# Turning each token tile's table places into integers one tile at a time, in an attention and mixture-of-experts kernel

## The chip, the cores and the metric

The kernel runs on one core of a Trainium2 chip. The metric is the device time of one launch in microseconds (us), from inputs in DRAM to the output in DRAM. The engines are TensorE (PE in the profile; its weight loads are shown apart as PEld), VectorE (DVE), ScalarE (ACT), GpSimd (POOL) and SyncE (SP). SP only issues transfers; POOL does a few element-wise steps and issues the indirect transfers, which are the scatters and gathers by a list of row numbers.

## What is computed

One transformer layer over x of shape (2, 1024, 256), all in float32: cross-attention to 154 context rows with 16 heads of 16, then a feed-forward with 8 experts, of which each token takes its two best.

```python
x = x + xattn(layernorm(x), ctx, ctx)          # 16 heads, softmax over 154 keys, then @ Wo + bo
z = layernorm(x)
probs = softmax(z @ router_w.T)                # 8 experts
vals, idx = top_k(probs, 2)
for e in range(8):
    w = sum(where(idx == e, vals, 0))          # 0 for tokens that did not choose e
    y = gelu(z @ w1[e].T) @ w2[e].T            # 256 -> 1024 -> 256
    out += w[:, None] * y
x = x + out
```

The kernel computes an expert only for the tokens that chose it.

## The kernel before

The 2048 tokens are 16 token tiles of 128, kept as four blocks n = 0..3 of four tiles i = 0..3 (TB = 4). The attention goes block by block; the expert stage goes over expert tiles j, each of which holds up to 128 (token, choice) pairs of one expert. There are 36 unconditional expert tiles (NI) and three more behind a test at the end.

**A written order.** The work is cut into small parts, generators such as `maxima(n, k)` or `expand(j, half)`, and every `yield` ends a piece of one. The string ORDER (lines 45 to 131) names the parts one after the other; each time a name comes up, that part goes on by one piece (line 1115). The instruction order of PE, DVE, ACT and SP is the order in which ORDER issues them. POOL's is too, until the part `release`; after it the scheduler of the framework chooses POOL's order. A queue is worked off in order, so an instruction that waits holds up all behind it on its own engine.

**Attention of one block**: `maxima` (PE scores, DVE row maxima, line 621), `drop` (DVE transposes the maxima, line 635; SP writes them to DRAM and from there into q, lines 638 and 641), `exps` and `last_exps` (PE scores, ACT exponentials, lines 653 to 674), `values` (PE, then a DVE transposition, line 695), `divide` (DVE reciprocal, product, transposition, lines 702 to 712), `project` (PE by Wo, DVE addition, SP store to out), `second_moments`, `second_scale`, `second_norm` (DVE, ACT, and an SP store of the normed rows to `x2n_d`).

**Routing of one block**: `logits` (PE, DVE, ACT), `share` and `choose` (DVE ranks the experts of each token), `place(n)` (PE counts the tokens ahead, DVE computes for each token and choice a row number in a table, lines 832 to 847). At its end `place` turns all eight row numbers per partition of the block into integers with one instruction (line 845). `record(n, i)` (line 849) then issues, for token tile i, one scatter for each of the two choices: 128 entries of token number and weight go to rows of the table `tab_d` in DRAM (line 854). The sixteen records are 32 scatters.

**Experts**: `plan(1)` counts after blocks 0 and 1 how many tiles each expert surely has, and with that fixes tiles 0 to 8; `plan(0)` fixes the rest after all blocks. Per tile j: `entries` (SP loads 128 table rows; it must follow the scatters), `fetch_weights` (SP, two loads of 512 KB), `fetch_rows` (POOL gathers the normed rows, line 973), `flip_rows` (PE transposes them, DVE copies, line 985), `expand` in two halves (PE, then gelu on ACT, line 1002), `contract` in two halves (PE, DVE weighting at line 1020, POOL scatter with addition into out, line 1023). The experts' second weights come by `load_w2(e)`, 1 MB each, on SP. After ORDER is used up, `tiles(0, NI)` issues what remains, tile by tile.

PSUM is shared: tag "one" has two buffers (among them those of logits, project, place, plan, values, flip_rows, contract), tag "two" has three (maxima, exps, last_exps, expand). A PE part can't begin before the buffer that it takes has been read out by DVE or ACT.

## Time and profile before

| what | value |
|---|---|
| median of 6 runs | 471.15 us (466.86 to 473.01) |
| profiled execution, its own time | 468.42 us |
| its span, first to last instruction | 466.7 us |
| granted PE clock, mean over the span | 0.961 |
| PE busy | 433.2 us (93%) |
| DVE, ACT, POOL busy | 169.6, 125.2, 149.2 us |
| scatters to the table (line 854) | 32, 975 ns each on POOL |
| integer conversions (line 845) | 4, 171 ns each |
| expand, contract on PE (lines 997, 1013) | 140.3 and 130.4 us in all |

A row of the timeline gives the start, the duration, the engine, the line, the operation, the tiles (out<-in) and how often; in brackets the idle time of that engine just before and what ended it. "remote" there means that the profile found no instruction that ended the wait. A row of the windows view gives, for a stretch of the span, each engine's busy time with its number of instructions, then the granted PE clock (1.00 is full speed), the share of the transfer engines and the rate.

### The profile page before, as it was taken

The numbers are of one execution on the slowest core, as the hardware profiler recorded it, in microseconds if no ns is written. First come the engines' busy times: TensorE is split into PE (matmuls) and PEld (weight loads), VectorE is DVE, ScalarE is ACT, GpSimd is POOL, SyncE is SP. The second block draws the span as 40 slices with busy tenths as digits, with TensorE's granted clock in tenths as the row PEclk, the third lists the DMA queues.
The fourth block names the chain that finished last, engine by engine and source line by source line (L and its number), as shares of the span: only waits on it lengthen the run. The fifth ranks groups of instructions, "written<-read, shape, count | busy, mean of one in ns | idle before, by whom it ended". The sixth has DMA issues, their size and how long they took to land. (4 is left out here: it accounts for less than half of the span.)

```text
span 466.7 us, 8169 instructions
## 1 busy us (share of the span) xinstructions
PE 433.2 (93%) x2992; PEld 334.9 (72%) x2992; DVE 169.6 (36%) x435; ACT 125.2 (27%) x206; POOL 149.2 (32%) x166
## 2 busy tenths in 40 slices
PE   7999999999985998979699999999999999999991
PEld 6554555344343427969699989999999999999990
DVE  6757766878842746631410111111111111111100
ACT  3275453441541450610111112111121111211210
POOL 5030242000075012466534334333343333432221
PEclk9999999999897598999999999999999999999997
DMA  8301222021714265968368765766656656662211
GB/s 268 132 8 27 86 97 95 9 93 46 305 27 91 73 199 158 249 117 308 47 176 258 213 197 141 200 163 182 207 136 196 174 161 208 148 192 25 23 14 13
DMA packets 32121, 63.75 MB, mean 137 GB/s; under 512 B 11929, under 2 KB 17617, under 8 KB 31057
## 3 DMA queue, kind: packets, MB, share of 16 engines
q1 hardware_dynamic: 23664, 54.19, 36.6%
q0 software_dynamic: 7936, 8.43, 10.8%
q8 instruction: 26, 0.43, 0.4%
q10 hardware_dynamic: 481, 0.58, 0.4%
q14 instruction: 14, 0.11, 0.1%
HBM read 54.63 MB, written 9.60 MB: 138 GB/s over the span
## 5 line engine op out<-in xcount | busy, mean ns | idle before, releaser
L997 PE MATMUL hp<-xgT,w 128*128 128x128 f32 x1152 | 140.3, 280 | 8.3 <-DVE xgT L985 4.7
L997 PEld LDWEIGHTS hp<-xgT,w 128*128 128x128 f32 x1152 | 137.6, 195 | 11.9 <-DVE xgT L985 5.9
L1013 PE MATMUL yp<-w_sb,hT 128*128 x576 | 130.4, 379 | 0.0
L1013 PEld LDWEIGHTS yp<-w_sb,hT 128*128 128x128 f32 x576 | 106.7, 190 | 13.1
L1002 ACT ACTIVATE hT<-hp 128x512 f32<-128x512 f32 x72 | 42.5, 597 | 224.7 <-issue 105.1
L1023 POOL DMA_INDIRECT out_dram<-ag,ents x36 | 57.2, 1589 | 106.4 <-DVE ag L1020 88.3
L973 POOL DMA_INDIRECT xg<-x2n_d,ents x36 | 38.0, 1055 | 85.9 <-PE xgt L982 48.2
L621 DVE TENSOR_REDUCE nmx<-mx 128x4 f32<-128x616 f32 x64 | 48.5, 793 | 32.2 <-PE mx L614 20.4
L1020 DVE TENSOR_SCALAR ag<-yp,ents 128x256 f32<-128x256 f32 x36 | 17.4, 483 | 114.5 <-PE yp L1013 78.5
L985 DVE COPY xgT<-xgt 128x256 f32<-128x256 f32 x36 | 15.2, 423 | 106.3 <-PE xgt L982 96.8
L854 POOL DMA_INDIRECT tab_d<-entry,rows_i x32 | 31.2, 975 | 37.6 <-issue 34.6
L659 ACT ACTIVATE et<-st 128x1024 f32<-128x1024 f32 x32 | 31.7, 1024 | 42.7 <-PE st L653 37.4
L614 PE MATMUL mx<-kaug,q 32*128 32x154 f32 x512 | 33.5, 330 | 9.0 <-issue 5.2
L614 PEld LDWEIGHTS mx<-kaug,q 32*128 32x128 f32 x512 | 23.7, 192 | 24.5 <-issue 11.3
L653 PE MATMUL st<-q,kaug 32*128 32x512 f32 x128 | 23.2, 665 | 0.4 <-DVE nmx L621 0.4
L684 PE MATMUL av<-er,vrem 128*128 128x512 f32 x32 | 19.7, 701 | 0.0
L596 POOL TENSOR_TENSOR x_sb<-x_sb,bo 128x1024 f32<-128x1024 f32 x4 | 9.4, 2356 | 27.0 <-DVE bo L548 25.9
L689 PE MATMUL av<-et,vaug 128*32 128x512 f32 x128 | 17.9, 633 | 0.0
L721 PE MATMUL op<-wo,catT 128*128 128x256 f32 x64 | 17.5, 422 | 0.0
L668 PE MATMUL sr<-q,krem 128*128 128x512 f32 x32 | 17.4, 672 | 0.0
L982 PE MATMUL xgt<-ident,xg 128*128 128x128 f32 x72 | 13.8, 273 | 2.6 <-DMA xg<-x2n_d,ents 2.6
L354 PE MATMUL qp<-w_sb,wq 128*128 128x512 f32 x32 | 16.0, 623 | 0.0
(169 smaller groups left out, 273.7 us busy)
## 6 DMA issues: line engine op xcount, KB each, us to landing
w<-in_w_dram SPq DMA_DIRECT2D x72, 512.0 KB
w_sb<-in_w_dram SPq DMA_DIRECT2D x8, 1024.0 KB
out_dram<-x_sb SPq DMA_DIRECT2D x8, 256.0 KB
x2n_d<-x2n SPq DMA_DIRECT2D x8, 256.0 KB
x_sb<-in_x_dram SPq DMA_DIRECT2D x3, 512.0 KB
ents<-tab_d SPq DMA_DIRECT2D x36, 1.0 KB
xg<-x2n_d,ents POOLq DMA_INDIRECT x36
out_dram<-ag,ents POOLq DMA_INDIRECT x36
```

What stands on the lines that cost most here:

```text
L614: nc.tensor.matmul(sc[j // 2][:, j % 2, gg * SC : (gg + 1) * SC], q[r, gg, i * P : (i + 1) * P], kaug[r, b, 2 * c + gg, :], start=True, st ...
L621: nc.vector.tensor_reduce(out=nmx[c][:, i, 0 : 2 * QJ].rearrange("p (g j) -> p j g", g=2)[:, pair * 2 : pair * 2 + 2, :], in_=sc[pair][:, ...
L653: nc.tensor.matmul(st[j // 2][:, j % 2, :], kaug[r, b, g, 0:SM], q[r, g % 2, :], start=True, stop=True)
L659: nc.scalar.activation(et, st[pair], AF.Exp)
L684: nc.tensor.matmul(av, vrem[:, b, g].rearrange("p j k -> p (j k)"), state["er", n, half][:, gg, :], start=True, stop=False,)
L689: nc.tensor.matmul(av[j * QR : (j + 1) * QR, :], vaug[:, b, g, j, :], state["et", n, g, j // 2][:, j % 2, :], start=False, stop=True,)
L854: ins = nc.gpsimd.indirect_dma_start(out=tab_d, out_offset=bass.IndirectOffsetOnAxis(ap=rows_i[:, i, k : k + 1], axis=0), in_=entry[:, n * ...
L973: nc.gpsimd.indirect_dma_start(out=xg[j % 3], out_offset=None, in_=x2n_d[0 : reach(j), :], in_offset=row_of(j), bounds_check=reach(j) - 1, ...
L997: nc.tensor.matmul(hp[:, q, :], w1t[dc][:, hc * P : (hc + 1) * P], xgT[:, dc, :], start=dc == 0, stop=dc == DC - 1,)
L1002: nc.scalar.activation(hT[:, half * (HC // 2) : (half + 1) * (HC // 2), :], hp, AF.Gelu)
L1013: nc.tensor.matmul(yp, hT[:, hc, :], flat[:, bass.ds(e * (HC * D) + hc * D, D)], start=hc == 0, stop=hc == HC - 1,)
L1023: nc.gpsimd.indirect_dma_start(out=out[0 : reach(j), :], in_=ag[j % 3], in_offset=None, out_offset=row_of(j), bounds_check=reach(j) - 1, o ...
```

## The change

`place` no longer converts the row numbers. Each `record(n, i)` begins with a DVE instruction of its own that converts the two row numbers of its token tile, and ends with the two scatters as before; the tile of unconverted numbers gets two buffers. There are thus 16 small conversions for 4 larger ones, and each has a place of its own in ORDER. All parts stand in a new order. The names and numbers of the other parts and their computation stay the same. Of the two ORDER strings, the stretches around the records are shown; in the new one a record appears twice, first for its conversion, then for its scatters.

```diff
@@ -43,91 +43,93 @@
 ORDER = """
...
-second_norm.0 maxima.3.3 drop.3.0 last_exps.2.1 last_exps.2.1 load_w2.6 exps.2.3 load_w2.7
-values.2.2 load_w2.4 share.1 second_norm.0 share.1 exps.2.3 drop.3.0 place.0 record.0.0 share.1
-exps.2.3 values.2.2 choose.1 values.2.3 choose.1 place.1 exps.3.0 values.2.3 record.0.1
-record.0.2 second_scale.1 last_exps.3.0 exps.3.0 exps.3.0 last_exps.3.0 divide.2.1 divide.2.1
-maxima.3.4 project.2.0 record.0.3 place.1 maxima.3.4 second_norm.1 project.0.1 maxima.3.5
-record.1.0 maxima.3.4 project.2.0 second_norm.1 project.2.1 maxima.3.5 maxima.3.6 maxima.3.5
-second_moments.2.0 add_bias.3 record.1.1 second_moments.2.0 project.2.1 plan.1 maxima.3.6
-maxima.3.6 project.1.1 second_norm.0 exps.3.1 exps.3.1 second_moments.2.1 record.1.2 maxima.3.7
-second_moments.2.1 second_norm.0 second_norm.1 second_scale.2 project.2.0 second_norm.1
-maxima.3.7 project.2.1 second_scale.2 record.1.3 second_norm.2 maxima.3.7 second_norm.2
-second_norm.2 exps.3.1 drop.3.1 drop.3.1 second_norm.2 plan.1 values.3.0 values.3.0 values.3.1
-logits.2 plan.1 fetch_weights.0 logits.2 exps.3.2 exps.3.2 values.3.1 exps.3.2 last_exps.3.1
-entries.0 entries.1 logits.2 exps.3.3 divide.3.0 last_exps.3.1 fetch_rows.0 exps.3.3 values.3.2
-exps.3.3 values.3.3 values.3.2 fetch_rows.1 divide.3.0 entries.4 flip_rows.0 flip_rows.0
-values.3.3 divide.3.1 logits.2 entries.6 divide.3.1 fetch_weights.1 entries.3 expand.0.0
-flip_rows.1 expand.0.1 expand.0.1 entries.8 project.3.0 entries.2 share.2 share.2 fetch_rows.3
-entries.5 flip_rows.1 share.2 fetch_rows.2 project.3.0 logits.3 expand.1.0 expand.1.0
-flip_rows.2 logits.3 choose.2 project.3.1 fetch_weights.2 flip_rows.2 choose.2 expand.0.0
-entries.7 project.3.1 second_moments.3.1 contract.0.0 second_moments.3.0 contract.0.1 place.2
-project.3.0 second_moments.3.1 fetch_weights.3 second_moments.3.0 expand.1.1 second_scale.3
-fetch_weights.7 contract.0.1 second_scale.3 second_norm.3 flip_rows.3 place.2 expand.2.0
-logits.3 logits.3 record.2.0 share.3 second_norm.3 record.2.1 expand.2.1 share.3 share.3
...
+choose.0 choose.0 last_exps.2.0 values.1.3 maxima.2.4 flip_half.3.0 maxima.2.4 maxima.2.5
+flip_half.3.1 flip_half.3.0 maxima.2.5 maxima.2.5 maxima.2.6 maxima.2.6 place.0 place.0
+record.0.0 maxima.2.6 record.0.0 flip_half.3.1 add_bias.1 exps.2.1 prep_q.3.0 exps.2.1
+divide.1.1 exps.2.1 prep_q.3.0 divide.1.1 maxima.2.7 maxima.2.7 maxima.2.7 drop.2.1 project.1.0
+project.1.0 prep_q.3.0 second_moments.1.0 second_moments.1.0 maxima.3.0 values.2.0 maxima.3.0
+project.0.0 maxima.3.1 maxima.3.0 maxima.3.1 record.0.1 project.1.1 maxima.3.1 values.2.0
+project.1.1 drop.2.1 exps.2.2 logits.1 exps.2.2 second_norm.0 second_moments.1.1 maxima.3.2
+exps.2.2 second_moments.1.1 values.2.1 second_scale.1 logits.1 maxima.3.2 maxima.3.3 logits.1
+load_w2.5 maxima.3.2 record.0.1 record.0.2 values.2.1 maxima.3.3 maxima.3.3 divide.2.0 logits.1
+last_exps.2.1 drop.3.0 divide.2.0 prep_q.3.1 share.1 share.1 exps.2.3 load_w2.6 record.0.2
+record.0.3 last_exps.2.1 values.2.2 second_scale.1 drop.3.0 share.1 values.2.2 second_norm.0
+prep_q.3.1 exps.2.3 choose.1 prep_q.3.1 exps.2.3 second_norm.1 values.2.3 choose.1 place.1
+exps.3.0 place.1 record.0.3 values.2.3 exps.3.0 exps.3.0 record.1.0 add_bias.2 divide.2.1
+divide.2.1 last_exps.3.0 maxima.3.4 record.1.0 second_norm.0 last_exps.3.0 maxima.3.4
+own_logits.3 own_logits.3 maxima.3.5 second_norm.1 load_w2.1 maxima.3.4 maxima.3.5 maxima.3.5
+record.1.1 project.1.0 project.2.0 project.2.0 maxima.3.6 maxima.3.6 plan.1 exps.3.1 record.1.1
+maxima.3.6 plan.1 logits.2 exps.3.1 maxima.3.7 project.2.1 maxima.3.7 maxima.3.7 add_bias.3
+record.1.2 drop.3.1 second_norm.1 second_moments.2.0 load_w2.3 logits.2 project.2.1
+second_moments.2.0 exps.3.1 values.3.0 second_moments.2.1 second_moments.2.1 values.3.0
+second_scale.2 second_scale.2 record.1.2 second_norm.1 load_w2.7 second_norm.2 values.3.1
+drop.3.1 exps.3.2 values.3.1 record.1.3 second_norm.2 second_norm.2 logits.2 exps.3.2 exps.3.2
+last_exps.3.1 plan.1 last_exps.3.1 second_norm.2 record.1.3 exps.3.3 fetch_weights.0 exps.3.3
+logits.2 divide.3.0 values.3.2 exps.3.3 entries.0 divide.3.0 fetch_rows.0 values.3.3 entries.2
+fetch_rows.2 entries.1 values.3.2 values.3.3 divide.3.1 entries.8 entries.6 divide.3.1 share.2
+share.2 project.3.0 fetch_rows.1 project.3.1 project.3.0 share.2 flip_rows.0 flip_rows.0
+project.3.1 entries.3 entries.7 fetch_weights.2 entries.5 choose.2 choose.2 expand.0.0
+fetch_rows.3 place.2 place.2 flip_rows.2 record.2.0 expand.0.1 project.0.1 entries.4 flip_rows.2
+record.2.0 logits.3 expand.0.1 second_moments.3.0 second_moments.3.0 logits.3 expand.2.0
+flip_rows.1 second_moments.3.1 second_moments.3.1 expand.0.0 fetch_weights.1 fetch_weights.3
+expand.2.1 second_scale.3 logits.3 record.2.1 second_scale.3 logits.3 share.3 second_norm.3
+second_norm.3 contract.0.0 flip_rows.1 plan.1 contract.0.1 contract.0.1 share.3 project.1.1
+flip_rows.3 expand.2.0 expand.2.1 record.2.1 second_norm.3 second_norm.3 record.2.2 record.2.2
+expand.1.0 flip_rows.3 fetch_weights.4 share.3 fetch_rows.4 record.2.3 choose.3 expand.1.1
+contract.2.0 contract.2.1 choose.3 project.3.0 fetch_rows.5 expand.3.0 expand.1.0 expand.1.1
+contract.2.1 contract.1.0 fetch_weights.8 flip_rows.4 contract.1.1 flip_rows.4 contract.1.1
+expand.3.1 place.3 fetch_rows.7 record.2.3 place.3 expand.4.0 plan.0 fetch_weights.5 flip_rows.5
+flip_rows.5 expand.3.0 fetch_weights.7 expand.4.0 expand.4.1 plan.0 fetch_rows.8 expand.3.1
+contract.0.1 flip_rows.7 contract.3.0 record.3.0 contract.3.1 fetch_weights.6 expand.4.1
+record.3.0 record.3.1 expand.5.0 flip_rows.7 expand.5.1 contract.4.0 expand.5.0 contract.4.1
+contract.3.1 project.3.1 expand.7.0 fetch_rows.6 contract.1.1 flip_rows.6 plan.0 expand.5.1
+expand.7.1 project.2.0 record.3.1 contract.2.1 record.3.2 flip_rows.6 plan.0 contract.4.1
+expand.7.1 contract.5.0 flip_rows.8 fetch_weights.11 contract.5.1 contract.5.1 expand.7.0
+record.3.2 fetch_weights.9 expand.6.0 record.3.3 contract.7.0 record.3.3 entries.9 contract.3.1
+expand.6.1 contract.4.1 entries.11 expand.6.0 flip_rows.8 entries.14 entries.16 fetch_rows.9
+contract.7.1 expand.8.0 expand.8.1 expand.8.0 contract.7.1 contract.6.0 expand.6.1 contract.6.1
+entries.12 fetch_weights.10 contract.6.1 expand.8.1 contract.8.0 flip_rows.9 contract.8.1
+flip_rows.9 entries.10 contract.5.1 expand.9.0 fetch_rows.10 expand.9.0 contract.8.1 entries.13
...
 """
@@ -839,28 +841,27 @@
         row = work.tile(shape, F32, tag="row", name=f"row{n}", bufs=1)
         nc.vector.tensor_tensor(row, pp, first.unsqueeze(1).to_broadcast(shape), ALU.add)
         nc.vector.tensor_tensor(one, one, row.unsqueeze(2).to_broadcast(each), ALU.mult)
-        rows = work.tile([P, TB, TOPK], F32, tag="rows", name=f"rows{n}", bufs=1)
+        rows = work.tile([P, TB, TOPK], F32, tag="rows", name=f"rows{n}")
         nc.vector.tensor_reduce(out=rows, in_=one, axis=AX.X, op=ALU.add)
-        rows_i = work.tile([P, TB, TOPK], I32, tag="rows_i", name=f"rows_i{n}")
-        nc.vector.tensor_copy(rows_i, rows)
-        state["rows", n] = rows_i
+        state["rows", n] = rows, work.tile([P, TB, TOPK], I32, tag="rows_i", name=f"rows_i{n}")
         yield
 
     def record(n, i):
 
-        rows_i = state["rows", n]
-        if i < TB:
-            for k in range(TOPK):
-                ins = nc.gpsimd.indirect_dma_start(
-                    out=tab_d,
-                    out_offset=bass.IndirectOffsetOnAxis(ap=rows_i[:, i, k : k + 1], axis=0),
-                    in_=entry[:, n * TB + i, k, :],
-                    in_offset=None,
-                )
-
-                tc.declare_no_dep(ins.ins, group="table", reason="distinct rows")
-                tc.add_to_no_dep_group("table", ins.ins)
-            yield
+        rows, rows_i = state["rows", n]
+        nc.vector.tensor_copy(rows_i[:, i, :], rows[:, i, :])
+        yield
+        for k in range(TOPK):
+            ins = nc.gpsimd.indirect_dma_start(
+                out=tab_d,
+                out_offset=bass.IndirectOffsetOnAxis(ap=rows_i[:, i, k : k + 1], axis=0),
+                in_=entry[:, n * TB + i, k, :],
+                in_offset=None,
+            )
+
+            tc.declare_no_dep(ins.ins, group="table", reason="distinct rows")
+            tc.add_to_no_dep_group("table", ins.ins)
+        yield
 
     done = const.tile([1, E + 1], F32, name="done")
```

## Prediction

> **What bounds the kernel now.** I read the page first, then stretches of the span, then the timeline where the stretches lose time, then the waits.
>
> ```profile
> PE 433.2 (93%) x2992; PEld 334.9 (72%) x2992; DVE 169.6 (36%) x435; ACT 125.2 (27%) x206; POOL 149.2 (32%) x166
> PEclk9999999999897598999999999999999999999997
> ```
>
> PE is the bound: 93% busy, its clock below full only in places. The stretches tell where. Columns: busy us of PE, PEld, DVE, ACT, POOL, clock, transfer share, GB/s.
>
> ```profile
> 116.70:140.00 23.30, 21.87 (x124) 9.30 (x122) 14.98 (x44) 11.35 (x17) 9.29 (x10) 0.93 0.45 166
> 140.00:163.40 23.40, 16.79 (x74) 8.77 (x74) 11.85 (x30) 6.78 (x13) 6.50 (x7) 0.65 0.31 82
> 210.00:233.40 23.40, 19.76 (x122) 17.93 (x122) 7.44 (x27) 2.88 (x5) 14.12 (x13) 0.96 0.59 177
> 280.00:303.40 23.40, 23.40 (x167) 22.16 (x167) 2.73 (x6) 3.94 (x7) 9.36 (x7) 1.00 0.62 170
> ```
>
> From 233 us on PE never rests; nothing in ORDER can be won there. The loss lies between 120 and 230 us, where routing is done. The timeline there, first around the first sixteen scatters, then around the last eight:
>
> ```profile
> 127.97 1.20 POOL L854 DMA_INDIRECT tab_d<-entry,rows_i  x1 [24.42 <-issue]
> 129.56 0.72 DVE L695 STREAM_TRANSPOSE u<-av 128x512 f32<-128x512 f32 x1 [1.74 <-PE av L689]
> 143.32 1.55 DVE L621 TENSOR_REDUCE nmx<-mx 128x4 f32<-128x616 f32 x2 [8.17 <-remote]
> 148.71 0.96 POOL L854 DMA_INDIRECT tab_d<-entry,rows_i  x1 [0.30 <-issue]
> 151.33 1.51 DVE L621 TENSOR_REDUCE nmx<-mx 128x4 f32<-128x616 f32 x2 [3.55 <-remote]
> ...
> 213.73 1.00 POOL L854 DMA_INDIRECT tab_d<-entry,rows_i  x1 [2.63 <-DVE rows_i L845]
> 219.60 0.48 DVE L1020 TENSOR_SCALAR ag<-yp,ents 128x256 f32<-128x256 f32 x1 [1.31 <-issue]
> 222.61 0.96 POOL L854 DMA_INDIRECT tab_d<-entry,rows_i  x1 [0.30 <-issue]
> 226.60 0.42 DVE L985 COPY xgT<-xgt 128x256 f32<-128x256 f32 x1 [6.52 <-remote]
> 226.62 0.60 ACT L1002 ACTIVATE hT<-hp 128x512 f32<-128x512 f32 x1 [13.45 <-remote]
> 227.08 2.05 PE L997 MATMUL hp<-xgT,w 128*128 128x128 f32 x16 [3.50 <-DVE xgT L985]
> ```
>
> POOL issues the scatters without a pause, one in 1.26 us, in three trains: 16 from 127.97, 8 from 195.66, 8 from 213.73. Early in a train DVE starts at once when PE has ended (129.56; 219.60, after five scatters). Later, DVE and ACT wait for matmuls that had long been recorded: at 143.32 for scores whose last row ends at 137.3, at 226.60 for a transposition begun at 221.19. The waits end 3 us after the train (208.7 after 205.5; 226.6 after 223.6) and there is no "remote" wait of this length elsewhere in the expert stage. Eight scatters are thus over 13.0 us after the first began (195.66 to 208.7), some 1.6 us each: more slowly than they are issued. I read this as a backlog that holds up PE's signals. That is inference; the trace names no cause.
>
> How much it costs: start to start, where nothing waits, a part takes PE 1.79 us (expand), 1.73 (contract), 2.05 (values), 1.92 (project), 1.91 (last_exps), 1.07 (exps), 0.78 (maxima), 0.57 (logits), 0.46 (place), 0.22 (flip_rows), 0.23 (plan). From maxima.3.3 (121.42) to expand.5.0 (227.08) PE has 10, 8, 6, 4, 3, 5, 5, 2, 3, 6 and 2 of these: 71.0 us of work in 105.7, so 34.7 us are lost. About 27 of them lie at the trains; the rest is 3.6 us before the first transposed rows (176.54), 1.7 at the half clock after it, and some 2 at 123.
>
> **The change, part by part.** The sum goes against the profiled execution, 468.42 us (span 466.7, 1.7 around it); the median of the runs is 471.15, 2.7 above it.
>
> *Conversions.* 4 of 0.17 us go, 16 come; 12 x (0.17 + 0.02 between) = 2.3 us more on DVE, 36% busy. Five of them (0.3 to 1.3) lie in the DVE queue ahead of a PE part and are in the terms below; the others are covered by PE work. The Trainium skill (Perfetto Trace Analysis, section Optimizing Scalar/DVE Operations) says to group small operations where the engine is saturated, each having an overhead of about 60 ns; it speaks against the split, and by its figure, as an estimate, the twelve cost 0.7 us; the rows' 2.3 decides.
>
> *Scatters.* Still 32, still 0.96 us each. By the part costs PE has 9.3, 7.2, 4.9, 5.6, 4.0, 7.3, 5.2 us of work from one conversion to the next over records 0.0 to 1.3; at 1.6 us a scatter a pair is over in 3.3. So the 34.7 us go. Ends: nothing is gained (the third rival), or all. I take all, because the first five scatters of a train delay nobody. Late pairs stand closer (2.1 to 2.3 within 5.5 us, 3.0 and 3.1 within 1.7): 0 to 5.9 (what the second train costs: 3.9 at it, 2.0 behind), taken 2.0.
>
> *New waits of the new order*, each with its ends and what I take:
> - place.1 needs choose.1, late in a full DVE queue (conversion 0.3 in it): 0.2 to 1, 0.6.
> - values.3.0 takes the PSUM buffer that DVE empties in logits.2, now behind place.1, values, divide, eight maxima, project, plan, drop and three conversions: 14 us of DVE rows from place.1 on, while PE has 12.3. 1.7 to 4, 2.2. Queued behind on DVE are the second moments, for which ACT waits.
> - exps.3.2 needs q by way of DRAM. On SP load_w2.7 now stands before drop.3.1. In the trace a drop behind loads took 2.79 us from its first store to the next (124.49 to 127.28) against 1.85 (160.42 to 162.27): 0.9; ends 0 and 3.4 (1 MB at the page's 305 GB/s).
> - values.3.2 behind ACT's norm, two exps and last_exps: 0 to 1, 0.3.
> - project.3.0 stands directly behind values.3.3. DVE must transpose, invert, multiply, transpose: 0.71 + 0.34 + 0.69 + 0.71, with handovers 2.6; before, 4.0 us of PE work covered it. No doubt about this one: 2.5 to 2.7.
> - flip_rows.0: from the plan's integers (164.99) to PE (176.54) it took 11.6 us by SP, the table rows, POOL and the gather. The plan's step now comes behind record.1.3; with the waits above its integers are ready at 142.2 on PE's count of work and PE arrives at 154.0: covered, if only just. With the wait for the copy (0.52 before): 0.5 to 2.5, 0.5.
> - flip_rows.9 needs the last scatter, its table rows (233.12 to 236.48) and a gather (3.5 to land); record.3.3 stands 14.0 us of PE work ahead, the chain is 11.2 plus the landing of the scatter, unseen, with two scatter-adds of 1.6 on POOL between: 0 to 3.5, 1.0. flip_rows.10 is similar and hides behind it.
> - The attention stage up to 120 us has the same parts and about the same DVE load in another order: -2 to 2, 0.
> - Clock. In 123.00 to 126.40 the windows view gives 0.50 although PE was busy 3.17 of 3.40 us just before, with small maxima; so the new waits and maxima in a row can bring such windows too, 1.7 us each. None to four, two taken: 3.4. The Trainium skill (TensorE: Matmul & The Clock Gate, section HAM oscillation) warns only of idle gaps above some 3.4 us; by that rule the term would be 0, and the row at 123 speaks against it.
>
> Moved loads (load_w2 on SP, x2 earlier) are covered: the last one ends before contract.0.0 needs it by over 15 us of PE work. POOL's bias additions (2.4 us each) come before its scatters, as POOL is idle then; uncovered, each would cost up to 2.4.
>
> Sum: 2.0 + 0.6 + 2.2 + 0.9 + 0.3 + 2.6 + 0.5 + 1.0 + 0 + 3.4 = 13.5. 468.42 - 34.7 + 13.5 = 447.2; with 2.7 for the median 450. With all low ends (2.9) 439, with all high ends (33) 469.
>
> **The rivals.**
> - *Late trains stay* (the change does only half of what it says). After `release` ORDER doesn't set POOL's queue; a pair held behind a gather can meet the next, and records 2 and 3 run together. For it: closeness of 2.1 to 2.3. Then 3.9 + 2.0 + 3.6 us come back for the 2.0: 447.2 + 7.5 + 2.7 = 457.
> - *The new order's own waits take the gain back*: first and ninth gather chains late, each some 5 us more, with DVE's queue at its high end: 466 to 474. Against it: each has cover in the count above.
> - *Slower: the price hangs on each scatter, not on the train.* A pair then holds up the attention stage, where all engines wait for PE. Spread, the 27 us are 0.85 a scatter, 1.7 a pair: 447.2 - 2 + 27 + 2.7 = 475. If the whole 3.3 us of a pair is exposed, 16 pairs cost 52: 500. Above 1.75 us a pair it is slower than before by over 1%. Against it stand the rows at 129.56 and 219.60.
>
> **How the numbers follow.** Forecast 0.60 (own range 439 to 469), late trains 0.12, gain taken back 0.10, price per scatter 0.16, the rest 0.02. Within 1% (466.4 to 475.9) is what a measurement of this kernel can hardly tell from no change. Faster: 0.60 + 0.12 less 0.03 for the forecast's top end, 0.69. Same 0.13, slower 0.18. Range 440 to 475: about 0.04 lies below, 0.16 above.
>
> **What would show it.** Right: scatters in pairs over some 95 to 230 us; no "remote" wait above 2 us on DVE or ACT; PE's idle time at line 614 gone; the clock near 1.00 from 140 to 163; first flip_rows near 165 us and not 176.5, though 3.8 us more PE work stands ahead of it; project.3.0 with a wait of 2.6. Wrong: DVE waits of several us inside single pairs; POOL with six or more scatters in a row; PE waits at line 982 on gathers.

## The result: not faster

The kernel after takes 472.39 us (median of 20 runs, 471.03 to 477.7); the kernel before beside it 471.94 (46 runs, 463.5 to 475.83). The medians are 0.1% apart; the ratio of undisturbed runs is 1.0113, with a 95% interval of 1.0079 to 1.0148, but of the kernel before it counts only the 12 of 46 runs that lie within 1.5% of its fastest. So the change is worth between nothing and a loss of 1.1% here. Forecast were 450 us and a faster kernel.

One thing must be known to read the experiments. The kernel before, the same file, takes about 471 us on some occasions and 448 to 452 on others; on chip number 15 it took 451 once and 472 another time. Within each of the sets of 7 to 18 runs beside the experiments it stays within 1.4%. I call the two sorts of occasion the 471 sort and the 450 sort. Every experiment is compared by its ratio to the kernel before beside it. On the 450 sort the change is 4.2% slower.

### The profile page after: what moved, and what is told of

Read it like the earlier page. It is cut to its first block, busy times and chain, and to the rows that moved or that the text cites. A ratio compares the mean times of both kernels' runs of the same rounds, so it can differ in the third digit from the quotient of the medians.

```text
span 471.7 us, 8180 instructions
## 1 busy us (share of the span) xinstructions
PE 430.5 (91%) x2992; PEld 333.4 (71%) x2992; DVE 172.4 (37%) x447; ACT 125.5 (27%) x206; POOL 148.8 (32%) x166
## 5 line engine op out<-in xcount | busy, mean ns | idle before, releaser
L998 PEld LDWEIGHTS hp<-xgT,w 128*128 128x128 f32 x1152 | 135.6, 193 | 5.4 <-DVE xgT L986 2.1
L998 PE MATMUL hp<-xgT,w 128*128 128x128 f32 x1152 | 137.0, 276 | 2.2 <-DVE xgT L986 1.4
L1014 PE MATMUL yp<-w_sb,hT 128*128 x576 | 135.5, 389 | 0.4 <-issue 0.2
L1014 PEld LDWEIGHTS yp<-w_sb,hT 128*128 128x128 f32 x576 | 109.2, 195 | 14.8 <-issue 0.8
L1021 DVE TENSOR_SCALAR ag<-yp,ents 128x256 f32<-128x256 f32 x36 | 17.4, 483 | 119.6 <-PE yp L1014 100.9
L655 PE MATMUL st<-q,kaug 32*128 32x512 f32 x128 | 23.3, 707 | 12.0 <-DMA q<-nm_d 11.9
L616 PEld LDWEIGHTS mx<-kaug,q 32*128 32x128 f32 x512 | 21.9, 188 | 15.1 <-issue 7.6
L616 PE MATMUL mx<-kaug,q 32*128 32x154 f32 x512 | 30.4, 323 | 0.5 <-DVE q L363 0.2
L655 PEld LDWEIGHTS st<-q,kaug 32*128 32x128 f32 x128 | 6.8, 206 | 22.9 <-issue 8.6
L598 POOL TENSOR_TENSOR x_sb<-x_sb,bo 128x1024 f32<-128x1024 f32 x4 | 9.4, 2356 | 35.7 <-issue 33.9
L686 PE MATMUL av<-er,vrem 128*128 128x512 f32 x32 | 17.9, 640 | 0.7 <-DVE lc L581 0.7
L723 PE MATMUL op<-wo,catT 128*128 128x256 f32 x64 | 15.8, 390 | 2.1 <-DVE catT L714 2.1
```

What stands on the lines that cost most here:

```text
L616: nc.tensor.matmul(sc[j // 2][:, j % 2, gg * SC : (gg + 1) * SC], q[r, gg, i * P : (i + 1) * P], kaug[r, b, 2 * c + gg, :], start=True, st ...
L655: nc.tensor.matmul(st[j // 2][:, j % 2, :], kaug[r, b, g, 0:SM], q[r, g % 2, :], start=True, stop=True)
L686: nc.tensor.matmul(av, vrem[:, b, g].rearrange("p j k -> p (j k)"), state["er", n, half][:, gg, :], start=True, stop=False,)
L998: nc.tensor.matmul(hp[:, q, :], w1t[dc][:, hc * P : (hc + 1) * P], xgT[:, dc, :], start=dc == 0, stop=dc == DC - 1,)
L1014: nc.tensor.matmul(yp, hT[:, hc, :], flat[:, bass.ds(e * (HC * D) + hc * D, D)], start=hc == 0, stop=hc == HC - 1,)
```

## The profile after

The profiled execution of the kernel after took 473.49 us (span 471.7), that of before 468.42. From the page, the engines and the clock:

```profile
PE 430.5 (91%) x2992; PEld 333.4 (71%) x2992; DVE 172.4 (37%) x447; ACT 125.5 (27%) x206; POOL 148.8 (32%) x166
PEclk9999999999799889998998899999999999999997
```

PE is as busy as before; the span is longer, so it waits longer. The windows view has the same four stretches as the prediction's (busy us of PE, PEld, DVE, ACT, POOL, clock, transfer share, GB/s):

```profile
116.70:140.00 23.30, 18.30 (x116) 7.23 (x117) 14.38 (x44) 9.30 (x15) 5.51 (x6) 0.85 0.55 135
140.00:163.40 23.40, 17.52 (x154) 9.08 (x152) 17.24 (x52) 7.95 (x13) 6.25 (x8) 0.96 0.65 178
210.00:233.40 23.40, 19.51 (x121) 17.33 (x120) 6.46 (x26) 2.98 (x6) 10.24 (x10) 0.93 0.69 185
280.00:303.40 23.40, 23.40 (x164) 22.08 (x163) 3.15 (x7) 4.18 (x7) 8.21 (x7) 1.00 0.63 174
```

The stretch of the first train did get better: 154 matmuls for 74 from 140 us on, the clock 0.96 for 0.65. But the stretch ahead of it got worse, 18.30 us busy for 21.87. What PE waits for, in all (us in total, times, longest), from the waits view:

```profile
PE st L655 <- DMA q<-nm_d: 11.9, 3, 5.2
PE xgt L983 <- DMA xg<-x2n_d,ents: 9.4, 3, 3.8
PE op L723 <- DVE catT L714: 2.1, 1, 2.1
```

Before, PE never waited for q. The timeline shows where the first of these waits comes from, and in its lower half the longest wait for a gather. In a row: start, duration, engine, line, operation, tiles; SPq is a transfer that SP issues.

```profile
89.16 0.32 SPq L640 DMA_DIRECT2D nm_d<-nmT  x1
90.83 1.15 SPq L643 DMA_DIRECT2D q<-nm_d  x2
...
105.55 1.20 POOL L855 DMA_INDIRECT tab_d<-entry,rows_i  x1 [10.65 <-issue]
107.05 0.97 POOL L855 DMA_INDIRECT tab_d<-entry,rows_i  x1 [0.30 <-issue]
109.52 0.32 SPq L640 DMA_DIRECT2D nm_d<-nmT  x1
114.24 0.96 POOL L855 DMA_INDIRECT tab_d<-entry,rows_i  x1 [6.23 <-DVE rows_i L852]
116.92 1.14 SPq L643 DMA_DIRECT2D q<-nm_d  x2
119.69 2.09 PE L655 MATMUL st<-q,kaug 32*128 32x512 f32 x8 [4.71 <-DMA q<-nm_d]
...
237.19 0.16 DVE L852 CAST rows_i<-rows 128x2 int32<-128x2 f32 x1
242.84 1.58 POOL L1024 DMA_INDIRECT out_dram<-ag,ents  x1 [3.01 <-issue]
244.72 0.99 POOL L855 DMA_INDIRECT tab_d<-entry,rows_i  x1 [0.30 <-issue]
248.32 3.69 SPq L951 DMA_DIRECT2D ents<-tab_d  x5
251.82 1.04 POOL L974 DMA_INDIRECT xg<-x2n_d,ents  x1 [4.82 <-DMA ents<-tab_d]
256.31 0.41 PE L983 MATMUL xgt<-ident,xg 128*128 128x128 f32 x2 [3.78 <-DMA xg<-x2n_d,ents]
```

A drop stores the row maxima to DRAM (line 640), waits until they have landed, and issues two transfers into q (line 643). With no scatter near, the step takes 1.67 us (89.16 to 90.83). With the second scatter of the first pair issued 2.5 us before the store it takes 7.40 (109.52 to 116.92), although no load is in flight. The trace's semaphore events say more: the store's bytes moved from 110.3 to 110.7, but its sixteen completions came from 113.19 to 116.79, right behind those of the pair's second scatter (113.01 to 115.67). PE waits for q and then runs at half clock from 117.0 to 123.8.

The lower half: the last conversion runs at 237.19, but POOL's queue holds its pair behind scatter-adds until 244.72; table rows and gather follow, and PE waits at 256.31. Of long "remote" waits, of which before had eight from 0.94 to 13.45 us, only two above 1 us are left: 7.8 on DVE and 4.43 on ACT, both where three pairs are issued close together, from 222 to 231.

## The experiments

Two theories. **T**, the forecast's: bunched scatters hold up PE's signals; spaced pairs don't. **W**: each scatter's writes to DRAM are slow to land, in pairs as in trains, and what must land in DRAM behind them is late too; the new order put stores that PE needs behind pairs. Labels that begin with a_ are edits of the kernel after, with b_ of the kernel before.

### No scatters for blocks 0 and 1: a_none, b_none

```diff
-        for k in range(TOPK):
+        for k in range(TOPK if n > 1 else 0):
```

> The kernel after, but the sixteen scatters of blocks 0 and 1 are left out (the conversions stay; the tables of the first nine expert tiles stay empty, so their gathers bring no rows). Only the span up to the first flip_rows is read. Theory W (writes): the three waits of exps for q (4.7 us at 114.98, 2.0 at 136.32, 5.2 at 156.70 in the kernel after) come from scatters: the store of the maxima to DRAM took 1.6 us to the next step of its drop where no scatter was near (89.16 to 90.83) and 7.4, 4.4 and 7.1 us where a pair stood just before it. Without scatters the first two waits fall below 0.5 us each, the third to at most 3.5 us (a load of 1 MB still stands before it), and PE comes to the first flip_rows 8 to 13 us earlier. Rival Q (queue): the waits come from where the drops stand in SP's order, behind stores and loads; then all three stay within 1 us of their sizes.

> The kernel before, but the sixteen scatters of blocks 0 and 1 are left out (their tables stay empty). Only the span up to the first flip_rows is read. Theory T (the forecast's reading: the train of scatters holds up DVE and ACT): the DVE waits of 8.2 and 3.6 us at 143.32 and 151.33 go, and PE, which lost 20 us between maxima.3.3 (121.42) and logits.2 (164.95), loses less than 5 there. Rival N (the waits have nothing to do with scatters): both waits stay and PE loses 15 us or more.

The timeline of a_none, first and last of its late drops:

```profile
112.44 0.32 SPq L636 DMA_DIRECT2D nm_d<-nmT  x1
114.09 1.14 SPq L639 DMA_DIRECT2D q<-nm_d  x2
...
146.40 0.32 SPq L636 DMA_DIRECT2D nm_d<-nmT  x1
150.87 1.15 SPq L639 DMA_DIRECT2D q<-nm_d  x2
```

Without scatters the step takes 1.65 us, and PE doesn't wait there. The last drop still takes 4.47, behind the load of 1 MB; with the pair it took 7.05. So W holds and Q falls: of the third drop's delay some 2.8 us are the load's and 2.6 the pair's. PE reached flip_rows.0 at 169.3 for 179.0 in the kernel after, 9.7 us earlier, within the 8 to 13 expected (in after_again, on the same sort of occasion as a_none, it was 177.8).

In b_none DVE has no long waits. Its timeline, row maxima 3 us apart:

```profile
138.80 1.51 DVE L618 TENSOR_REDUCE nmx<-mx 128x4 f32<-128x616 f32 x2
141.88 1.50 DVE L618 TENSOR_REDUCE nmx<-mx 128x4 f32<-128x616 f32 x2
```

By the part costs of the prediction PE loses 2.6 us between maxima.3.3 and logits.2, for 19.9 in before. But the kernel before beside it took 449, not 471, so a second profile of before was needed. That profile (next section) has no long DVE waits either, with all its scatters; so b_none speaks neither for T nor against it.

### The same two kernels once more: before_again, after_again

> The kernel before itself, with a profile. Beside the first four experiments it took 445.6 to 451.8 us, beside the kernel after 463.5 to 475.8. Reading V1: what the trains of scatters cost differs from one occasion to the next; if it is near 449 again, PE loses under 8 us between maxima.3.3 and logits.2 (19.9 in the profile of before) and the DVE wait of 8.2 us is below 3. Reading V2: the difference lies elsewhere (clock, loads, expert stage); then PE loses 15 us or more there whatever the time.

> The kernel after itself, beside the kernel before on the same chip as the other runs of this call. If the cost of scatters differs by the occasion alike for both orders, the ratio is 1.00 to 1.02 again. If only bunched scatters differ (V1), and the kernel before takes about 449, the kernel after stays at 465 to 473 because its waits for q and its late gathers do not hang on bunching, ratio 1.035 to 1.05.

before_again took 452.21; after_again 468.91 beside 451.09, ratio 1.0418 (1.0362 to 1.0475). V1 holds in the main: the ratio lies in its range, and the DVE wait is gone, but the loss between maxima.3.3 and logits.2 is still 9.2 us, not below 8. No wait in before_again is put down to "remote", though sixteen scatters go in a row as ever. What is left of the train's price is W's, at another store. Its timeline:

```profile
146.05 0.32 SPq L755 DMA_DIRECT2D x2n_d<-x2n  x1
...
154.64 1.09 ACT L750 ACTIVATE x2n<-x_sb,off,r 128x256 f32<-128x256 f32 x2 [5.77 <-DMA x2n_d<-x2n]
...
156.69 1.07 PE L689 MATMUL av<-et,vaug 128*32 128x512 f32 x2 [6.77 <-ACT et L659]
```

The store of normed rows at 146.05, in the middle of the train, has landed by 154.6; the one at 126.50 took 2.7 us. ACT needs the buffer back, its exponentials stand behind, and PE stands behind those. The kernel after has its own waits on both sorts of occasion (12.1 us for q here, 11.9 in the first profile).

### Pairs moved off the drops: a_pairs, a_pairs2

```diff
 a_pairs: one word each, the next record's conversion behind it
-place.0 place.0 record.0.0 maxima.2.6 record.0.0
+place.0 place.0 maxima.2.6 record.0.0
...
-maxima.3.0 maxima.3.1 record.0.1 project.1.1
+maxima.3.0 maxima.3.1 record.0.0 record.0.1 project.1.1
...
-record.0.1 record.0.2 values.2.1 ... record.0.2 record.0.3
+record.0.1 values.2.1 ... record.0.2 record.0.2 record.0.3
...
-add_bias.3 record.1.2 drop.3.1 ... second_moments.2.1 values.3.0 second_scale.2
+add_bias.3 drop.3.1 ... second_moments.2.1 values.3.0 record.1.2 second_scale.2
```

> The kernel after with three conversions moved: record.0.0's stands directly before record.0.1's (behind drop.2.1), record.0.2's before record.0.3's (behind drop.3.0), record.1.2's behind values.3.0 (behind drop.3.1). Theory W: no pair is issued in the few us before a store of the maxima, so the waits of exps.2.2 and exps.3.0 for q (4.7 and 2.0) fall below 1 us each, that of exps.3.2 falls by 1 to 3 us, and half-clock windows of 3.4 us go with them; some 8 to 11 us less at the first flip_rows and 461 to 466 us at the end. Rival Q (the drops' place in SP's order): the waits keep their sizes, and the time stays at 470 to 474. A third possibility, that four scatters in a row bring the waits of DVE back, would show as DVE waits of several us behind them and a time above 470 with the q waits gone.

It took 470.55 beside 449.43, ratio 1.0489 (1.0401 to 1.0576), no less than the kernel after (1.0418); the gain that W gave it didn't come. The edit did less than the text says: of record.0.0 only the second word, the issue, moved; its conversion stayed ahead of drop.2.1. POOL issued the pair at 105.96 as before. That makes the kernel a comparison within itself. Its timeline, the three late drops:

```profile
109.36 0.32 SPq L636 DMA_DIRECT2D nm_d<-nmT  x1
116.31 1.14 SPq L639 DMA_DIRECT2D q<-nm_d  x2
...
128.86 0.33 SPq L636 DMA_DIRECT2D nm_d<-nmT  x1
130.55 1.14 SPq L639 DMA_DIRECT2D q<-nm_d  x2
...
148.77 0.32 SPq L636 DMA_DIRECT2D nm_d<-nmT  x1
158.89 1.15 SPq L639 DMA_DIRECT2D q<-nm_d  x2
```

The first, still behind a pair, took 6.95 us; the second, now ahead of its pair, 1.69 (4.35 in the kernel after); the third, behind eight scatters since 131.5, 10.12. a_pairs2 moved conversion and issue both:

```diff
 a_pairs2: both words of each record, put behind
+maxima.3.1 record.0.0 record.0.0 ... values.2.0 record.0.1 record.0.1
...
+share.1 record.0.2 record.0.2 ... values.2.2 record.0.3 record.0.3
...
+values.2.3 record.1.0 record.1.0 ... values.3.0 record.1.1 record.1.1
...
+values.3.1 record.1.2 record.1.2 ... logits.2 record.1.3 record.1.3
```

> The kernel after with the pairs of blocks 0 and 1 taken out of the way of the three late drops, now for conversion and issue both: 0.0 and 0.1 behind drop.2.1, 0.2, 0.3 and 1.0 behind drop.3.0, 1.1 to 1.3 behind drop.3.1. (In a_pairs only the issue word of 0.0 had moved, so drop.2.1 still stood behind a pair.) Theory W: the drops' stores land in 1.4 us as in a_none (1.65 us from store to q transfer), drop.3.1's in 4.5 because of the load before it; the waits of exps.2.2 and exps.3.0 fall below 0.5 us each, that of exps.3.2 below 3; the first flip_rows comes 7 to 11 us earlier than in the kernel after and the time is 5 to 10 us below the kernel after's. Rival: the waits move on to the next store or gather behind the pairs (stores of normed rows, table loads, the first gather), and the time falls by less than 3 us although the q waits are gone.

471.12 beside 451.09, ratio 1.0445 (after_again 1.0418 on the same chip). The theory's number was wrong, the rival right: the waits move on. From the waits view:

```profile
PE xgt L979 <- DMA xg<-x2n_d,ents: 13.0, 3, 6.6
PE st L651 <- DMA q<-nm_d: 7.7, 2, 6.5
```

drop.2.1's wait is gone, but drop.3.0 now stands behind the four scatters that were put off (6.5 us), drop.3.1 waits 1.2 for 6.4, and gathers behind later scatters wait 13.0 for 7.3. There is no free place for sixteen slow scatters among stores and gathers that PE needs.

### The pairs alone, in the old order: b_pairs

```diff
 kernel before, with the conversion in record as in the kernel after
-... values.2.3 record.0.1 record.0.2 second_scale.1 ...
+place.0 record.0.0 ... values.2.3 record.0.1 ... divide.2.1 record.0.2
+maxima.3.5 record.0.3 ... project.2.1 record.1.0 ... second_moments.2.1 record.1.1
+values.3.0 record.1.2 ... values.3.1 record.1.3
```

> The kernel before in its own order of parts, with one conversion for each token tile (16 for 4) and the pairs of blocks 0 and 1 spread over the stretch from place.0 to values.3.1, those of blocks 2 and 3 converted where the scatters' words stand. Theory T alone: only bunched scatters cost; the waits at the trains go (27 us of the 34.7) and the time is 443 to 453. Theory W (a scatter's writes land slowly, wherever it stands, and what is late is what must land behind it): the DVE waits shrink, but stores of the maxima and of rows behind pairs become late instead; 455 to 468. Rival N: 470 or more.

461.65 beside 449.43, ratio 1.0271 (1.0171 to 1.0372): within the 455 to 468 of W, on an occasion where trains cost no late signals. The spread pairs reach past drop.3.1: its store at 147.47 is followed by the q transfer at 157.00, and PE waits 4.8 us for ACT and 3.1 for q.

### The last conversions earlier: a_late

```diff
-project.2.0 record.3.1 contract.2.1 record.3.2 flip_rows.6 ... expand.6.0 record.3.3 contract.7.0 record.3.3 entries.9
+flip_rows.7 record.3.2 record.3.2 ... contract.4.0 expand.5.0 record.3.3 record.3.3 ... entries.9
```

> The kernel after with the conversions of record.3.2 and record.3.3 earlier in VectorE's order: 3.2 behind the copy of flip_rows.7, 3.3 behind expand.5.0's gelu, both ahead of the weighting of tiles 3 to 5. In the kernel after the last pair was converted at 237.19 and issued at 244.72, behind two scatter-adds that waited for VectorE; the table rows, the gather and flip_rows.9 followed at 248.3, 251.8 and 256.3, with PE waits of 3.8 and 2.6 us and two half-clock windows (3.4 us together). Theory: with the last scatter some 12 us earlier both waits and both windows go: 7 to 10 us less. Rival (eight scatters in a row bring the waits of the third train back, 3.6 us and more): 2 to 5 us less or none.

457.18 for after_again's 468.91 on the same chip: 11.7 us, more than the 7 to 10 expected. PE no longer waits for the late gathers; the q waits stay, 12.2 us in all. The rival's late signals didn't come, but this was the 450 sort of occasion.

### The drop without DRAM: a_sb, a_sb_late

```diff
-        nc.sync.dma_start(out=to, in_=nmT)
         for gg in range(2):
             row = (1 - gg) * DK
+            for a in range(QB):
+                first_row = a * QR + gg * QJ
-            nc.sync.dma_start(out=q[row::QR, gg, :]..., in_=to...)
+                nc.sync.dma_start(out=q[row::QR, gg, :]...[:, :, a], in_=nmT[first_row : first_row + QJ, :]...)
```

> The kernel after with the drop changed and nothing else: the transposed maxima go straight from SBUF into q in eight transfers of 8 KB, no longer by a store to DRAM and two transfers back. Theory W, sharpened: what lands late behind a scatter is what is written to DRAM; transfers that end in SBUF do not (in the kernel after the q transfers issued at 116.92, with a pair just ahead, were there in about 1 us, the store of 109.52 took 7.3). Then the waits of exps.2.2, exps.3.0 and exps.3.2 for q (4.5, 1.3 and 6.4 us in after_again) fall below 1 us each, half-clock windows go with them, and the first flip_rows is 10 to 15 us earlier; at the end 8 to 14 us below the kernel after. Price: eight issues of about 0.57 us on SP for three of 1.5 together, 3 us of SP a drop, which is off the path unless a drop becomes late. Rival: a scatter blocks the transfer engines or their queues as such; then the eight transfers are late too and the time is within 3 us of the kernel after.

Ratio 1.0185 (457.82 beside 449.32), for after_again's 1.0418: some 10 us. The waits view has one wait left of three:

```profile
PE st L651 <- DMA q<-nmT: 1.8, 1, 1.8
```

The pair was issued as before (104.00 and 105.49), and the completions of its second scatter came from 110.77 to 113.64. The eight transfers into SBUF, issued from 108.09 to 112.22, were late behind it too: the first of a transfer's five semaphore events came 0.95 us after its issue, but the last came from 112.42 to 113.81, after 4.3 us for the first transfer and 1.6 for the eighth, where each takes 1.6 with no scatter near (87.73 to 92.93 for all eight). The "about 1 us" of the expectation is that first event; by the last one the q transfer of 116.92 took 2.6. So the sharpened theory, that transfers into SBUF are not late, isn't shown. What the straight drop spares is a store that must land before the next issue: from its first issue until q is there it takes 5.7 us behind the pair for 5.2 undisturbed, the drop by way of DRAM 10.2 (109.52 to 119.75) for 4.2 (89.16 to 93.39).

> a_sb and a_late together: straight drops, and the last two conversions earlier. a_late took 11.7 us off the kernel after (457.2 for 468.9 on one chip). If the two waits are independent the sum is 20 to 26 us off the kernel after, 443 to 449 there, below the kernel before (451). If the gathers follow the last scatter and not PE, the second gain is partly swallowed: 450 to 456.

447.37, ratio 0.9957 (0.9922 to 0.9993): the two gains nearly add up, 4.6% of the kernel before together for 2.6 and 2.3 alone.

### Longer table rows: a_wide, b_wide

```diff
-    tab_d = dram.tile([(LAST + 1) * P, 2], F32, name="tab_d")
+    tab_d = dram.tile([(LAST + 1) * P, 16], F32, name="tab_d")
...
-                in_=entry[:, n * TB + i, k, :],
+                in_=entry[:, n, 2 * (i * TOPK + k) : 2 * (i * TOPK + k) + 16],
...
-        nc.sync.dma_start(out=ents[:, j, :], in_=tab_d[bass.ds(tile_ * P, P), :])
+        nc.sync.dma_start(out=ents[:, j, :], in_=tab_d[bass.ds(tile_ * P, P), 0:2])
```

> The kernel after with table rows of 64 bytes for 8 (an entry and the 14 numbers that follow it in SBUF; only the first two are read back), nothing else. If it is the short rows that make a scatter land slowly, a pair lands in 2 to 3 us where it took 4 to 9, the stores behind it in under 2 us, the waits for q fall below 1 us each except the one behind the load of 1 MB (about 3), and the time is 8 to 14 us below the kernel after. Rival: the cost is one of 128 rows at 128 places, whatever their length; landings and waits stay and the time is within 3 us of the kernel after.

> The kernel before with table rows of 64 bytes for 8, nothing else. On the chips where it takes about 450 its one large loss is behind the train of sixteen: a store of normed rows issued in it landed after 8.5 us (2.7 without scatters), ACT waited 5.8 for its buffer and PE 6.8 for ACT. If short rows are the cause: 440 to 446 where the kernel before takes 450; where it takes 471, far more, 445 to 455. Rival as for a_wide: within 2 us of the kernel before.

a_wide has the order of the kernel after and eight times the bytes, and took 451.92, ratio 1.0059 (1.0028 to 1.0091): 3.6% below after_again's ratio, some 16 us, more than the 8 to 14 expected. b_wide took 442.61, ratio 0.9829 (0.976 to 0.9898). In a_wide the first pair, issued at 108.33 and 109.82, had landed by 110.65 and 111.96; each scatter of b_wide's train of sixteen that shows all its events landed 2.1 to 3.4 us after its issue (the third: 131.52 to 133.62), where the second and third of before_again's took 8.5 and 8.0. What is left of the waits in a_wide:

```profile
PE xgt L981 <- DMA xg<-x2n_d,ents: 6.7, 1, 6.7
PE st L651 <- DMA q<-nm_d: 1.3, 1, 1.3
```

The q waits are gone but for the load's share; the one long gather wait is the late last scatter, which a_late removes. So the rows of 8 bytes were the cause of these waits. The edit makes a row longer and moves the rows of the table 64 bytes apart, both at once; which of the two counts no run separates. And the gain is one of the attention stage: in the expert stage, where weights are loaded, the scatters of b_wide's two trains of eight landed after 2.1 to 8.4 us, those of before_again's after 3.2 to 8.4.

### What the order and the spacing are worth: a_wide_late, a_bunched, a_wide_bunched

a_wide_late has the edits of a_wide and of a_late. a_bunched undoes the spacing of blocks 0 and 1 alone:

```diff
-place.0 place.0 record.0.0 maxima.2.6 record.0.0
+place.0 place.0 record.0.0 record.0.1 record.0.2 record.0.3 maxima.2.6 record.0.0
...
-exps.3.0 exps.3.0 record.1.0 add_bias.2
+exps.3.0 exps.3.0 record.1.0 record.1.1 record.1.2 record.1.3 add_bias.2
```

> The kernel after with table rows of 64 bytes and the two last conversions earlier (a_wide and a_late together). With the price of the short rows and the late last scatter both gone, what stays is the order itself. If the order and the pairs are worth something, 430 to 438, below b_wide (442.6 with the old order and whole trains). If the forecast gain was only ever in avoiding trains of short rows, 439 to 445, level with b_wide.

> The kernel after, but the four conversions of block 0 and those of block 1 stand together where the first of each stood, so that eight scatters go in a row twice; everything else in its place. The forecast's theory (only bunching costs): VectorE and ScalarE wait for recorded matmuls late in each train and PE loses 8 us or more against the kernel after: 476 to 485. Theory W (128 short rows cost the same wherever they stand; what counts is which store is behind them): drop.2.1 has a longer queue ahead of it (wait of exps.2.2 5 to 9 us for 4.5), drop.3.0 has none (wait below 0.5 for 1.3 to 2), drop.3.1 as before; within 5 us of the kernel after, either side.

These two met the 471 sort of occasion (before beside them 472.13); the numbers expected of a_wide_late were made for the other. a_wide_late took 449.79, ratio 0.9524 (0.9484 to 0.9565). a_bunched took 478.08, ratio 1.0119 (1.0046 to 1.0193). That ratio counts all seven runs of before beside it, so it can't be set beside the 1.0113 of the kernel after; by the medians a_bunched is 1.3% above its kernel before and the kernel after 0.1%, so that bunching costs some 4 to 6 us (the profiled executions differ by 3.5). Its timeline in the first train of eight:

```profile
107.81 0.32 SPq L636 DMA_DIRECT2D nm_d<-nmT  x1
...
115.34 1.51 DVE L619 TENSOR_REDUCE nmx<-mx 128x4 f32<-128x616 f32 x2 [3.57 <-remote]
115.78 1.14 SPq L639 DMA_DIRECT2D q<-nm_d  x2
...
121.08 2.09 PE L651 MATMUL st<-q,kaug 32*128 32x512 f32 x8 [7.81 <-DMA q<-nm_d]
```

Both theories show at once. T: DVE waits 3.57 us here and 4.42 in the second train for matmuls long recorded. W: the q wait of exps.2.2 grows from 4.71 to 7.81, that of exps.3.0 vanishes, that of exps.3.2 falls from 5.19 to 1.08, because the drops now stand elsewhere against the scatters: 8.9 in all for 11.9. The sum is a loss: from place.0 to the first flip_rows PE loses 25.5 us, for 21.1 in the kernel after. T had the direction and the range of the time (476 to 485), but the loss came smaller than its 8 us or more; it lies at the edge of W's "within 5 us".

Do late signals hang on the short rows too? a_wide_late has eight scatters of 64-byte rows in a row from 203.78 to 212.71. Its timeline there:

```profile
207.34 0.60 ACT L1001 ACTIVATE hT<-hp 128x512 f32<-128x512 f32 x1 [2.68 <-remote]
...
216.74 0.42 DVE L984 COPY xgT<-xgt 128x256 f32<-128x256 f32 x1 [11.00 <-remote]
```

Not on them alone: on this sort of occasion the signals are late beside bunched scatters with long rows as well, and PE takes 7.0 us longer over the parts around them than in the same kernel on the other sort (a_wide_late2).

> b_wide once more (the old order, whole trains, table rows of 64 bytes), beside the new order with the same rows. Where the kernel before takes about 450, b_wide took 442.6; where it takes about 471, its trains of 8-byte rows also make VectorE and ScalarE wait for matmuls long recorded. If those waits too come from the short rows: 442 to 450 in either case and no wait of that kind over 1 us. If they come from sixteen scatters in a row whatever their rows: 455 to 470 on an occasion of the second kind.

> a_wide_late once more, beside b_wide: the new order with pairs against the old with trains, both with rows of 64 bytes, on one chip. If spacing or the new order is worth something with cheap scatters, a_wide_late is below b_wide by 4 us or more; if not, the two are within 4 us, or the old order is ahead.

> b_wide a third time, for an occasion on which the kernel before takes about 471. There: if the waits of VectorE and ScalarE for long-recorded matmuls in trains come from the short rows, 442 to 452 and no such wait over 1 us; if they come from sixteen scatters in a row whatever their rows, 455 to 470. On an occasion on which the kernel before takes about 450 it says only 442 to 445 again.

> a_wide_late with the four conversions of block 0, and those of block 1, together where the first of each stood (as a_bunched was to the kernel after): eight scatters of 64-byte rows in a row twice. If spacing is worth nothing once the rows are long, within 3 us of a_wide_late (440.8 where the kernel before takes 448, 449.8 where it takes 472). If bunching costs by itself, 5 us or more above it.

All four met the 450 sort. b_wide again: 444.85, ratio 0.9923 (0.9896 to 0.995), and as b_wide3 444.07, 0.9897 (0.9829 to 0.9964). a_wide_late again: 440.84, ratio 0.9838 (0.9786 to 0.9891), beside b_wide's 444.85 on one chip: 4.0 us. a_wide_bunched, which bunches blocks 0 and 1 of a_wide_late: 440.76, ratio 0.9839 (0.981 to 0.9868). So on that sort the spacing of blocks 0 and 1 is worth nothing once scatters land quickly, and the 4.0 us are not its doing. Whether whole trains of sixteen long rows delay signals on the 471 sort was not seen.

a_wide_late beats both kernels on both sorts of occasion.

## Why the prediction was wrong, point by point

PE's lost time by the part costs, in the old order from maxima.3.3 to expand.5.0, in the new from place.0 to flip_rows.11 (two parts there, prep_q, have no cost in the prediction and are taken at 1.92 us):

| | old order | new order |
|---|---|---|
| 8-byte rows, 471 sort | 34.7 (before) | 39.7 (after) |
| 8-byte rows, 450 sort | 16.4 (before_again) | 35.7 (after_again) |
| 64-byte rows, 450 sort | 10.0 (b_wide) | 17.4 (a_wide) |
| the same, last conversions earlier | | 8.5 (a_wide_late2) |

Read down: the 471 sort adds 18.3 us in the old order and 4.0 in the new (I call this late signals, as the "remote" waits stand only there); short rows cost 6.4 and 18.3; the rest 10.0 and 17.4. The change thus gains 14.3 and loses 11.9 and 7.4: 5.0 us slower, where the two profiled executions differ by 5.07. By the medians they differ by 0.45 only; the profiled execution of before lies 3.5 us below its median, that of after 1.1 above. The terms come from different occasions, so each is good to a few us.

- *Scatters: "at 1.6 us a scatter a pair is over in 3.3. So the 34.7 us go."* This step failed. It gave the whole loss to late signals and put nothing for what must land in DRAM behind a pair. That trains hold up PE's signals was right, as a_bunched shows, but only on one sort of occasion, and it owned 18.3 of the 34.7, of which the change gained 14.3. Another 10.0 stay with long rows (b_wide), and 8.9 even without the scatters of blocks 0 and 1 (b_none); 6.4 were the price of short rows, which in the new order is 18.3, because stores and gathers that PE needs stand behind the pairs. The rows at 129.56 and 219.60 showed only that DVE wasn't held up early in a train; they said nothing of what must land. And 1.6 us is about the pace at which scatters land one behind the other, not the time after which one has landed: the second of the first pair landed 8.6 us after its issue, and the fifteen of before_again's sixteen whose events the trace shows in full landed some 1.5 us apart, but 5.5 to 11.2 us after their issue. (POOL did pause once in before's first train, 1.64 us ahead of 142.40; nothing hangs on it.)
- *"The attention stage up to 120 us has the same parts": 0 (-2 to 2).* Failed: drop.2.1 stands behind pair 0.0. 4.7 us of wait and 2.1 at half clock up to 123.86, of which PE waits through the beginning, make 6.8. For exps.3.0, 2.0, there was no term at all.
- *exps.3.2: 0.9 (0 to 3.4).* Measured 5.2 and two windows. The load was the right suspect for 2.8 us of the late drop (a_none), the pair in front for 2.6.
- *project.3.0: 2.6.* Measured 2.1. *values.3.0: 2.2.* Measured 0.7. *place.1, values.3.2:* no wait above 0.5. *flip_rows.0: 0.5.* Measured 0.5 for the copy. *Conversions:* DVE was busy 2.8 us longer (172.4 for 169.6), for 2.3.
- *flip_rows.9: 1.0 (0 to 3.5); flip_rows.10 "hides behind it".* Measured 3.8 and 2.6, with two windows. The chain was taken as 11.2 us from the last conversion; it was 19.1 (237.19 to 256.31). Of that 7.5 is POOL's queue: the two scatter-adds that I counted at 1.6 each stand ahead of the pair, and each was issued only when the scatter-add before it had landed, not when VectorE was ready, as the expectation of a_late has it (that of 227.11 landed at 237.46, that of 238.22 at 242.08). a_late recovers 11.7.
- *Late pairs: 2.0 (0 to 5.9).* flip_rows.7 waits 3.0 for a gather issued at 205.50 behind four scatters; its landing took until 214.8. Where three pairs are issued from 222 to 231 the signals are late (4.43 on ACT, 7.8 on DVE).
- *Clock: two windows, 3.4.* Seven came in this stretch of the kernel after; PE waited through parts of two of them, so that they cost some 10.4. The Trainium skill (TensorE: Matmul & The Clock Gate, section HAM oscillation) ties them to idle gaps of PE above about 3.4 us. The gaps of 4.71 and 5.19 fit it; but windows also followed gaps of 2.98 and 2.61 us here, and in a_sb one of 1.83, and none followed the gap of 2.07 at 175.84.
- *The rivals.* "Its own waits take the gain back" (466 to 474) holds the measured 472.4, in part by luck: it is right for the ninth gather chain, but the first has no wait beyond the copy's 0.5, and it doesn't name q. "The price hangs on each scatter" (475) is nearest in kind, but was named at the wrong place, as DVE waits inside a pair. It is the landing, and it hangs on the short rows (a_wide).
- *What would show it:* all but two of the remote waits did go, the clock from 140 to 163 is near full, project.3.0 waits; the first flip_rows came at 179.0 and not near 165, and PE waits for gathers. The profile could have been asked what stands behind a scatter: in before's train the store of 147.80 landed after 5.8 us, the one of 157.02, behind the train, after 2.0; the lateness was hidden behind the late signals.

The Trainium skill (DMA: Bandwidth & Descriptors, section Specifications) says that transfers below 512 bytes are done by read-modify-write. By that line rows of 8 and of 64 bytes are of one kind. The runs tell them apart: with 8 bytes the second scatter of the first pair landed after 8.6 us, with 64 after 2.1 (a_wide). Whether read-modify-write is what makes the short rows slow no run shows.

## What to carry to other kernels

When indirect stores are moved, list what must land in DRAM within some 8 us behind each, and who waits for it; their own issue time says nothing about that. Before spacing small scatters, try longer rows: here 64 bytes for 8 were worth 16 us in one order and 3 to 8 in the other. And let the instruction that completes a long chain (the last scatter before a table is read) be issued as early as it can be, ahead of what waits in the same queue.

## What had not been expected of the hardware

- A store of 64 KB whose bytes had moved by 110.7 was signalled complete only from 113.19 to 116.79, behind a scatter of 1 KB; of eight transfers of 8 KB into SBUF at the same place in the order, the first was 2.7 us late and the last not at all (a_sb).
- In a train of sixteen in the attention stage, scatters of 128 rows of 64 bytes, issued every 1.26 us, landed after 2.1 to 3.4 us (b_wide), those of 8 bytes after 5.5 to 11.2 (before_again). Neither holds everywhere: in the expert stage both took up to 8.4, and the kernel after's last scatter, of 8-byte rows, landed after 2.3 (246.02).
- Beside bunched scatters DVE and ACT waited up to 13.45 us for matmuls long recorded. Such waits above 1 us stand in all four profiles taken on the 471 sort and in none of the sixteen on the 450 sort, for the same files and on chips of the same number; 64-byte rows don't cure it. Why is open.
- Half-clock windows of 3.4 us follow some PE gaps of 1.8 to 3 us too.
